# Attention scores of four images: from VectorE products to TensorE blocks with a masked sum, and a new order of an image's turn

## The chip, the cores and the metric

The kernel runs on one core of one Trainium2 chip. The metric is device time in microseconds (us) of one execution, the median over runs. In the text, PE is TensorE (PEld its weight loads), DVE is VectorE, ACT is ScalarE, POOL is GpSimd, SP is SyncE, which issues most transfers.

## The reference, cut to what matters

Four images of 784 patches become tokens of 256 features. The tokenizer puts the same tokens three times in a row (`REP = 3`). Then come two layers, each with an attention and a feed-forward part, all in float32. The change touches the attention of layer 0 alone. There the scores are taken between *images*, summed over all positions:

```python
mn = (m - mu) * jax.lax.rsqrt(var + EPS) * gamma + beta
q = (mn @ Wq).reshape(N, L, H, C)          # N images, L tokens, H = 8 heads of C = 32
k = (mn @ Wk).reshape(N, L, H, C)
v = (mn @ Wv).reshape(N, L, H, C)
g = jax.nn.sigmoid(mn @ Wg + bg).reshape(N, L, H, C)
att = jnp.einsum('slhc,tlhc->sth', q, k) * scale
att = jax.nn.softmax(att, axis=1)
o = jnp.einsum('sth,tlhc->slhc', att, v) * g
return o.reshape(N, L, H * C) @ Wo + bo
```

So for each pair of images (s, t) and each head, one number is the sum of 784 x 32 products. Behind it stand a mixture of six experts (two chosen for each token), a second attention and a second mixture.

## The kernel before, in words

**Stages.** The tokenizer runs first. Then, for eight groups `g` of three tiles of 128 tokens (group 0 has a fourth tile with the 16 left-over tokens of each image), `keys_values(g)` normalises the rows, turns them to features on partitions (`mT`), and projects them with `Wk` and `Wv`. After that each image `s` has a turn; the turns of images 0, 1 and 2 are a loop, image 3 is written out behind it. Then come the blocks of the experts (`hidden`, `rows_back`), the gathers, and layer 1.

**Order.** In these parts the order of PE, DVE and ACT is written by hand (`manual_schedule`): each engine works off its instructions in the program's order, and waits on semaphores for the other engines. PSUM tiles of one pool of seven banks are used in rotation.

**Keys and queries.** `projected(g, Wk, kT)` multiplies with a 128 x 128 piece of `Wk` as the stationary operand and 384 tokens as the moving one, so keys lie with features on partitions (`kT`, in the buffer `kq`). `q_mm` and `q_copy` do the same for the queries of one image, in halves of 392 tokens, two of them for each half `o` of the features (four heads each).

**Scores.** `products(s, o, ts)` multiplies on DVE the queries of image s with the keys of image t (128 x 784) and sums along the tokens by `accum_out`: one instruction for each o and t, 32 in all. `weights_of_images(s)` multiplies the sums by a matrix of head blocks on PE (tile `pl`), and makes the softmax over the images on DVE and ACT.

**A turn of image s.** `gate_mm` (16 PE records, tile `pg`) and `gate_act` make the gates with Tanh; `first_value` and `values` add up the weighted values of the four images on DVE into `oT`; `attended` projects pairs of tiles with `Wo` (tile `pwo`), adds them to the residual `h` on DVE and sums squares on ACT. The image before (u = s - 1) is routed in the same turn: `scales_of` (square root), `shifts_of`, `rows_of_part` (normalised rows `xn`), `turn_part` (12 transposes `pt`), `router` and `router_logits` (`pr`, `plg`), `choose` (18 small DVE instructions), `count` (`pcount`) and `send` (12 scatters on POOL). `mix1` to `mix3` belong to the image before that. The queries of image s + 1 are made in the turn of s.

**Behind it.** The expert weights `ew` (six transfers on SP, L1443) take the place of `kq` in SBUF, so they wait for the last reader of `kq`. `own_weights` copies one expert's weights out of `ew` (L1360) for each block of tokens.

**TensorE records.** A float32 matmul leaves two records in the trace, a transpose one.

Of the kernel before, what the change touches and what calls it, by code (L numbers as in the profile page):

```python
# [21 lines left out]
F32 = mybir.dt.float32  # L22
# [5 lines left out]
P = 128  # L28
# [18 lines left out]
PW = 4  # L47
SEG = 32
HALF = SEQ // 2
E0 = 6  # L50
E1 = 4
BLK = 256
# [16 lines left out]
def tile_vit_tower(ctx: ExitStack, tc: tile.TileContext, a: dict, out: bass.AP):  # L69
# [215 lines left out]
    def mm_t(n, w, wcols, xT, name, chunks=2):  # L285

        pm = ps_tile(name)
        for c in range(chunks):
            nc.tensor.matmul(  # L289
                pm[: wcols.stop - wcols.start, :n], w[:, c, wcols], xT(c),  # L290
                start=(c == 0), stop=(c == chunks - 1),
            )
        return pm[: wcols.stop - wcols.start, :n]
# [470 lines left out]
    scale = REP / math.sqrt(CHEAD) / math.sqrt(REP * SEQ)  # L764

    keys = layer0.enter_context(tc.tile_pool(name="keys", bufs=1, reuse_waits="tile"))
    kq = keys.tile([P, 2 * TOK + 4 * SEQ], F32, tag="kq", name="kq")
    kT = kq[:, : 2 * TOK].rearrange("p (c n) -> p c n", c=2)
    qT2 = kq[:, 2 * TOK :].rearrange("p (s c n) -> p s c n", s=2, c=2)
# [6 lines left out]
    pqs, pgs = {}, {}  # L776
    scatters = []

    def q_mm(s, o):
        if s >= NI:  # L780
            return
        pqs[s, o] = [
            mm_t(
                HALF, Wq, slice(o * P, (o + 1) * P),
                lambda c: mT[:, c, s * SEQ + i * HALF :][:, :HALF], "pq",
            )
            for i in range(2)
        ]

    def q_copy(s, o):  # L790
        if s >= NI:
            return
        if o == 0:
            qTs[s] = qT2[:, s % 2]
        for i, pq in enumerate(pqs.pop((s, o))):
            nc.scalar.copy(qTs[s][:, o, i * HALF : (i + 1) * HALF], pq)  # L796

    def gate_mm(s, o):
        pgs[s, o] = [
# [7 lines left out]
    def gate_act(s, o):  # L807
        gate = gates[s, o] = attr.tile([P, SEQ], F32, tag="gate", name="gate")
        for i, pg in enumerate(pgs.pop((s, o))):
            nc.scalar.activation(  # L810
                gate[:, i * HALF : (i + 1) * HALF], pg, AF.Tanh, bias=bgh[:, o : o + 1], scale=0.5
            )

    def products(s, o, ts=range(NI)):
        if s >= NI:
            return
        if s not in atts:
            atts[s] = small.tile([P, 2, NI], F32, tag="part", name="part")
        for t in ts:
            prod = attm.tile([P, SEQ], F32, tag="prod", name="prod")  # L820
            nc.vector.scalar_tensor_tensor(  # L821
                prod, qTs[s][:, o, :], 1.0, kT[:, o, t * SEQ : (t + 1) * SEQ],
                ALU.mult, ALU.mult, accum_out=atts[s][:, o, t : t + 1],
            )

    def weights_of_images(s):
        pl = psum_s.tile([P, 512], F32, tag="pss", name="pl")
        nc.tensor.matmul(
            pl[:, : 2 * NI], headmask, atts[s].rearrange("p o t -> p (o t)"),
            start=True, stop=True,  # L830
        )
# [12 lines left out]
    def first_value(s, o, n0, n, eng):  # L844
        if s not in oTs:
            oTs[s] = attr.tile([P, 2, SEQ], F32, tag="oT", name="oT")
        acc, v, w = oTs[s][:, o, n0 : n0 + n], vT[:, o, n0 : n0 + n], atts[s][:, o, 0:1]
        if eng is nc.scalar:
            nc.scalar.activation(acc, v, AF.Copy, scale=w)
        else:  # L850
            nc.vector.tensor_scalar(acc, v, w, None, ALU.mult)
# [358 lines left out]
    def projected(g, w, dst):  # L1210
        n = len(groups[g])
        t0 = groups[g][0]
        at = slice(t0 // TPI * SEQ + t0 % TPI * TT, t0 // TPI * SEQ + (t0 % TPI + 3) * TT)
        for o in range(2):
            pm = mm_t(
                n * TT, w, slice(o * P, (o + 1) * P),
                lambda c: firsts[0][:, c, :] if n > 3 else mT[:, c, at], "pkv",
            )
            nc.scalar.copy(dst[:, o, at], pm[:, : 3 * TT])  # L1219
            if n > 3:  # L1220
                nc.scalar.copy(left(dst[:, o, :]), left_of(pm[:, 3 * TT :]))

    def keys_values(g):
        projected(g, Wk, kT)
        if g + 2 < len(groups):
            stats = second_norm(g + 2)
        if g == 0:
            third[n - 1] = turned_rows(n - 1)
        turn_second(g + 1)
        projected(g, Wv, vT)  # L1230
        if g == 0:
            last_rows(n - 1)
        if g + 2 < len(groups):
            second_rows(g + 2, stats)

        t0 = groups[g][0]
        for ht, k in ((h[:, t0 : t0 + 3, :], 3), (h[:, LT:, :], 1))[: len(groups[g]) - 2]:
            nc.vector.tensor_tensor(ht, ht, over(bo, k), ALU.add)

    with tc.manual_schedule(engines=by_hand):  # L1240
        turn_second(0)
        last_rows(n - 2)
        second_rows(1, second_norm(1))
        keys_values(0)
        for g in range(1, len(groups)):
            keys_values(g)

            if g == 1:
                for o in range(2):
                    q_mm(0, o)  # L1250
                    q_copy(0, o)
            if g % 2 and g + 1 < len(groups):
                for o in range(2):
                    products(0, o, [g // 2])
    front.close()
    route = attention.enter_context(
        tc.tile_pool(name="route", bufs=1, side="right", reuse_waits="tile")
# [3 lines left out]
    with tc.manual_schedule(engines=by_hand):  # L1261
        for s in range(NI - 1):
            u = (s - 1, 0, TPI) if s else None
            past = (s - 2, 0, TPI) if s >= 2 else None
            if u:
                scales_of(u)
            if s == 0:
                for o in range(2):
                    products(0, o, [NI - 1])
                weights_of_images(0)  # L1270
            gate_mm(s, 0)
            gate_mm(s, 1)
            gate_act(s, 0)
            if s:
                products(s, 1, range(2))
            if u:
                shifts_of(u)
                rows_of_part(u)
                products(s, 1, range(2, NI))
            if s:  # L1280
                weights_of_images(s)
            if u:
                turn_part(u)
            first_value(s, 0, 0, SEQ, nc.vector)
# [149 lines left out]
    ew = keys.tile([P, E0, EW], F32, tag="kq", name="ew")  # L1434
# [817 lines left out]
```

## Time and profile before

| what | value |
|---|---|
| median of 3 runs | 784.22 us (781.89 to 785.8) |
| profiled execution: its time, its span | 785.9 us, 784.2 us |
| PE busy, DVE busy, ACT busy | 703.4, 480.2, 328.7 us |
| groups of keys and values | about 117 to 174.3 us of the span |
| turn of image 0, 1, 2 (first to last square root, `scales_of`) | from 174.3; 194.1 to 223.0; 223.0 to 253.7 |
| image 3 up to the first expert block | 253.7 to 286.0 us |
| expert blocks of layer 0 | 286 to 465 us |
| mean granted PE clock | 0.964 |

Starts in the trace are microseconds from the start of the span. "Busy" counts instructions at work; "idle before" is the wait of an engine in front of an instruction, with what ended it.

### The profile page before, as it was taken

What the parts mean: (1) busy time and instruction counts of PE and PEld (TensorE: products, weight loads), DVE (VectorE), ACT (ScalarE), POOL (GpSimd) and SP (SyncE); (2) the same over time, 40 slices, a digit from 0 to 9 for tenths busy, and PEclk for the clock granted to TensorE, in tenths of its full rate; (3) what the DMA queues carried; (4) which work ended last, traced back from release to release, by engine and by line L of the source; (5) the groups of instructions that cost most, each with busy time, mean ns of one, the idle gap of its engine ahead of it and who ended that gap; (6) DMA issues with size and microseconds to landing.
All of it is one profiled execution on the core that took longest, in us unless ns stands there. A gap on an engine that the chain in (4) does not pass through costs nothing.

```text
span 784.2 us, 10588 instructions
## 1 busy us (share of the span) xinstructions
PE 703.4 (90%) x3391; PEld 482.0 (61%) x3391; DVE 480.2 (61%) x1523; ACT 328.7 (42%) x777; POOL 129.2 (16%) x231
## 2 busy tenths in 40 slices
PE   6898899999888778998899999269999999999996
PEld 3745565666556456787788875146776775554653
DVE  4666886768778743446544766479965654454441
ACT  0545776455573652342222326135445613222221
POOL 5400000000064316500003027670000000000000
PEclk9999999999999789999999999779999999999999
DMA  8399999000021853432234252330000012223333
GB/s 189 99 415 418 418 415 416 6 1 1 0 82 40 289 187 110 141 94 76 88 95 121 94 156 75 88 100 8 1 0 1 1 24 93 82 63 102 104 112 105
DMA packets 56118, 96.24 MB, mean 123 GB/s; under 512 B 6376, under 2 KB 46031, under 8 KB 56063
## 3 DMA queue, kind: packets, MB, share of 16 engines
q1 hardware_dynamic: 49648, 79.38, 28.9%
q0 software_dynamic: 5536, 14.32, 6.0%
q10 hardware_dynamic: 878, 1.86, 1.0%
q8 instruction: 27, 0.44, 0.2%
q14 instruction: 29, 0.23, 0.1%
HBM read 30.45 MB, written 65.09 MB: 122 GB/s over the span
## 4 chain that ended last, share of the span: by engine, by line
PE 68%; DVE 16%; ACT 6%; issue 4%; DMA 3%; POOL 2%; DVEq 1%; ACTq 0%; another core or an unknown queue 0%; SPq 0%
PE pb L1384 11%; PE pe L289 6%; PE pyb L1402 5%; PE ps L289 4%; PE pqk L1828 4%; PE pkv L289 4%; PE pt L280 3%; PE pw L558 3%; PE pwp L300 3%; PE ps L2202 3%; PE pout L2002 2%; PE pout L2007 2%; DVE oT L856 2%; PE pukx L1927 2%; DMA img<-in_x_dram 2%
## 5 line engine op out<-in xcount | busy, mean ns | idle before, releaser
L1045 POOL DMA_INDIRECT xrows<-xn,pos x50 | 55.7, 1115 | 247.6 <-ACT kq L796 185.8
L1598 POOL DMA_INDIRECT ys<-yrows,pos x50 | 50.6, 1012 | 140.6 <-DMA yrows<-yb 123.9
L1384 PE MATMUL pb<-xTb,own 128*128 128x256 f32 (+1 forms) x240 | 56.0, 378 | 10.7 <-DVE own L1360 5.8
L1390 ACT ACTIVATE hb<-pb,own 128x256 f32<-128x256 f32 (+1 forms) x74 | 33.6, 456 | 62.7 <-PE pb L1384 50.4
L1384 PEld LDWEIGHTS pb<-xTb,own 128*128 128x128 f32 x240 | 42.3, 197 | 19.3 <-ACT hb L1390 8.5
L1384 PE MATMUL pb<-hb,own 128*128 128x256 f32 (+1 forms) x240 | 52.2, 360 | 0.8 <-DVE hb L1392 0.5
L1402 PE MATMUL pyb<-own,hb 128*128 128x256 f32 x216 | 52.6, 384 | 0.3 <-ACT hb L1390 0.2
L280 PE MATMUL pt<-ident,xn 128*128 128x128 f32 x200 | 34.8, 302 | 12.5 <-DVE xn L584 6.6
L289 PE MATMUL pe<-xT,eW 128*128 128x512 f32 (+1 forms) x112 | 46.0, 553 | 0.0
L1828 PE MATMUL pqk<-Wqkv,lxT 128*128 128x512 f32 x100 | 44.9, 594 | 0.2 <-ACT lxT L89 0.2
L1402 PEld LDWEIGHTS pyb<-own,hb 128*128 128x128 f32 x216 | 40.7, 193 | 6.5 <-ACT hb L1390 0.6
L1384 PEld LDWEIGHTS pb<-hb,own 128*128 128x128 f32 x240 | 40.5, 190 | 5.9 <-DVE hb L1392 1.2
L280 PEld LDWEIGHTS pt<-ident,xn 128*128 128x128 f32 x200 | 25.6, 151 | 28.2 <-ACT xn L919 8.5
L1408 DVE TENSOR_TENSOR yb<-pyb,eb 128x512 f32<-128x512 f32 (+1 forms) x30 | 19.1, 638 | 38.4 <-PE pyb L1402 28.1
L558 PE MATMUL pw<-Wall,pT 128*128 128x512 f32 x96 | 42.6, 593 | 0.0
L1373 ACT COPY xTb<-ptb 128x512 f32<-128x512 f32 (+1 forms) x30 | 16.2, 541 | 56.7 <-PE ptb L1369 49.9
L1392 DVE TENSOR_SCALAR hb<-pb,own 128x256 f32<-128x256 f32 (+1 forms) x46 | 20.6, 447 | 28.6 <-PE pb L1384 20.5
L1842 ACT ACTIVATE qk<-qk 128x256 f32<-128x256 f32 x50 | 20.4, 408 | 38.6 <-DVE qk L1834 35.0
L821 DVE SCALAR_TENSOR_TENSOR prod<-kq 128x784 f32<-128x784 f32 x32 | 30.4, 971 | 6.0 <-ACT kq L1219 3.4
L289 PEld LDWEIGHTS pe<-xT,eW 128*128 128x128 f32 x112 | 20.2, 190 | 21.6 <-issue 16.5
L1360 DVE COPY own<-ew 128x1540 f32 x30 | 28.9, 966 | 6.9 <-ACT xTb L1373 2.7
L1612 DVE SCALAR_TENSOR_TENSOR h<-ys,wk,h 128x256 f32<-128x256 f32 x50 | 23.5, 481 | 14.0 <-DMA ys<-yrows,pos 13.8
(414 smaller groups left out, 1463.5 us busy)
## 6 DMA issues: line engine op xcount, KB each, us to landing
xrows<-nothing SPq DMA_DIRECT2D x22, 896.0 KB
yrows<-nothing SPq DMA_DIRECT2D x22, 896.0 KB
out_dram<-h SPq DMA_DIRECT2D x23, 384.0 KB
xb<-xrows SPq DMA_DIRECT2D x24, 256.0 KB
yrows<-yb SPq DMA_DIRECT2D x24, 256.0 KB
ew<-in_L_ffn_expert_w_dram SPq DMA_DIRECT2D x6, 768.0 KB
wb<-wd SPq DMA_DIRECT2D x16, 128.0 KB
img<-in_x_dram SPq DMA_DIRECT2D x2, 588.0 KB
```

The lines of the kernel that those rows point to most:

```text
L280: nc.tensor.transpose(pt[:, j * TT : (j + 1) * TT], xn[:, j, c * P : (c + 1) * P], ident[:TT, :TT])
L289: nc.tensor.matmul(pm[: wcols.stop - wcols.start, :n], w[:, c, wcols], xT(c), start=(c == 0), stop=(c == chunks - 1),)
L300: nc.tensor.matmul(pm[:, i, :], xT(c, t), w[:, c, :], start=(c == 0), stop=(c == chunks - 1))
L558: nc.tensor.matmul(pm, pixels(c, tiles[j]), Wall[:, c, :], start=(c == 0), stop=(c == 1))
L821: nc.vector.scalar_tensor_tensor(prod, qTs[s][:, o, :], 1.0, kT[:, o, t * SEQ : (t + 1) * SEQ], ALU.mult, ALU.mult, accum_out=atts[s][:, o ...
L1045: put = nc.gpsimd.indirect_dma_start(out=xrows[:, :], out_offset=bass.IndirectOffsetOnAxis(ap=pos[:, k, t0 + j : t0 + j + 1], axis=0), in_ ...
L1360: nc.vector.tensor_copy(w, ewf[0][:, bass.ds(off, EW)])
L1384: nc.tensor.matmul(pm, wm[:, c, o * P : (o + 1) * P], src[:, c, :], start=(c == 0), stop=(c == 1),)
L1390: nc.scalar.activation(dst[:, o, :], pm, AF.Relu, bias=b)
L1402: nc.tensor.matmul(pm[:, t, :], src[:, c, t * P : (t + 1) * P], wm[:, c, :], start=(c == 0), stop=(c == 1),)
L1598: got = nc.gpsimd.indirect_dma_start(out=y[:, j, k, :], out_offset=None, in_=yrows[:, :], in_offset=bass.IndirectOffsetOnAxis(ap=pos[:, k, ...
L1828: nc.tensor.matmul(pqk, xTs[u][:, c, cut(j, 1)], Wqkv[:, c, : 2 * D], start=(c == 0), stop=(c == 1),)
```

## The change

Keys and queries are now made with *tokens* on partitions: seven chunks of 112 tokens for each image (`KC`, `NKC`), the chunk of `mT` as the stationary operand and the 256 columns of `Wk` or `Wq` as the moving one (`token_rows`). The scores become matmuls (`scores`): for each chunk and head, 32 columns of queries are stationary and the keys of all four images move (4 x 32 columns), so that PSUM holds a 32 x 32 block for each head and image t, of which only the diagonal is wanted. `score_sums` multiplies by a mask (`same`) and sums, on DVE. The loop's order is new: `weights_of_images(s)` stands behind the gate matmuls also for image 0, the queries of s + 1 stand ahead of the routing, `rows_of_part` shares its rows between ACT and DVE.

```diff
+KC = 112
+NKC = SEQ // KC
-    kq = keys.tile([P, 2 * TOK + 4 * SEQ], F32, tag="kq", name="kq")
+    kq = keys.tile([P, (NI + 1) * NKC * D], F32, tag="kq", name="kq")
+    def token_rows(s, ms, w, dst, name):
+        made = []
+        for m0 in ms[::2]:
+            two = [m for m in (m0, m0 + 1) if m in ms]
+            pm = ps_tile(name)[:KC].rearrange("p (t d) -> p t d", t=2)
+            for i, m in enumerate(two):
+                for c in range(2):
+                    nc.tensor.matmul(
+                        pm[:, i, :], mT[:, c, s * SEQ + m * KC :][:, :KC], w[:, c, :],
+                        start=(c == 0), stop=(c == 1),
+                    )
...
+    def scores(s):
+        ps = scored[s] = ps_tile("psc")[:, : 2 * NI * CHEAD]
+        for o in range(2):
+            for m in range(NKC):
+                for i in range(4):
+                    h0 = (4 * o + i) * CHEAD
+                    nc.tensor.matmul(
+                        ps[i * CHEAD : (i + 1) * CHEAD, o * P : (o + 1) * P],
+                        qrow[:, m, h0 : h0 + CHEAD], krow[:, :, m, h0 : h0 + CHEAD],
+                        start=(m == 0), stop=(m == NKC - 1),
+                    )
+    def score_sums(s):
...
+        nc.vector.tensor_tensor(own_, ..., same..., ALU.mult)
+        nc.vector.tensor_reduce(part.rearrange("p o t -> p (o t)"), own_, AX.X, ALU.add)
-    def products(s, o, ts=range(NI)):
...
     def keys_values(g):
-        projected(g, Wk, kT)
+        key_rows(g)
...
-            if g % 2 and g + 1 < len(groups):
-                for o in range(2):
-                    products(0, o, [g // 2])
+        scores(0)
+        score_sums(0)
...
             if u:
                 scales_of(u)
-            if s == 0:
-                for o in range(2):
-                    products(0, o, [NI - 1])
-                weights_of_images(0)
             gate_mm(s, 0)
             gate_mm(s, 1)
             gate_act(s, 0)
-            if s:
-                products(s, 1, range(2))
+            weights_of_images(s)
+            gate_act(s, 1)
             if u:
                 shifts_of(u)
-                rows_of_part(u)
-                products(s, 1, range(2, NI))
-            if s:
-                weights_of_images(s)
+                rows_of_part(u, both=True)
+            q_mm(s + 1, 0)
+            first_value(s, 0, 0, SEQ, nc.vector)
+            first_value(s, 1, 0, SEQ, nc.scalar)
+            q_copy(s + 1, 0)
             if u:
                 turn_part(u)
-            first_value(s, 0, 0, SEQ, nc.vector)
-            first_value(s, 1, 0, SEQ, nc.scalar)
-            gate_act(s, 1)
+            q_mm(s + 1, 1)
+            q_copy(s + 1, 1)
...
-            q_mm(s + 1, 0)
-            q_copy(s + 1, 0)
...
-            q_mm(s + 1, 1)
-            q_copy(s + 1, 1)
+            scores(s + 1)
             values(s, 1, 0, SEQ, range(1, 3))
...
             keep_left(s)
-            products(s + 1, 0, range(2))
-            for k, two in enumerate(halves(range(TPI))):
+            score_sums(s + 1)
+            for two in halves(range(TPI)):
                 attended(s, two)
-                if k < 2:
-                    products(s + 1, 0, [2 + k])
...
         gate_mm(s, 1)
         gate_act(s, 0)
-        products(s, 1, range(2))
+        weights_of_images(s)
         shifts_of(u)
         gate_act(s, 1)
-        products(s, 1, range(2, NI))
-        weights_of_images(s)
```

The queries of image 0 are still made behind group 1. `ew` takes the place of the smaller `kq`, whose last reader is now `scores(3)`, in the turn of image 2.

More of the change, by code (lines that the diff above doesn't have):

```diff
@@ L766, in tile_vit_tower @@
     keys = layer0.enter_context(tc.tile_pool(name="keys", bufs=1, reuse_waits="tile"))
-    kq = keys.tile([P, 2 * TOK + 4 * SEQ], F32, tag="kq", name="kq")
-    kT = kq[:, : 2 * TOK].rearrange("p (c n) -> p c n", c=2)
-    qT2 = kq[:, 2 * TOK :].rearrange("p (s c n) -> p s c n", s=2, c=2)
+    kq = keys.tile([P, (NI + 1) * NKC * D], F32, tag="kq", name="kq")
+    krow = kq[:KC, : NI * NKC * D].rearrange("p (t m d) -> p t m d", t=NI, m=NKC)
+    qrow = kq[:KC, NI * NKC * D :].rearrange("p (m d) -> p m d", m=NKC)
+    same = keys.tile([P, CHEAD], F32, tag="same", name="same")
+    nc.vector.tensor_reduce(
+        same, ident.rearrange("p (h c) -> p c h", c=CHEAD), AX.X, ALU.add
+    )
     att = ctx.enter_context(ExitStack())
@@ L775, in tile_vit_tower @@
     qTs, gates, atts, oTs, sums, rows0, turned0, logits0, picked, mixed = ({} for _ in range(10))
-    pqs, pgs = {}, {}
+    pqs, pgs, scored = {}, {}, {}
     scatters = []
-    def q_mm(s, o):
+    def token_rows(s, ms, w, dst, name):
[9 more added lines that the diff above has]
+                    )
+            made.append((dst[:, m0 : m0 + len(two), :], pm[:, : len(two), :]))
+        return made
@@ L780, in q_mm, with q_copy @@
+    def q_mm(s, part):
         if s >= NI:
             return
[L782 to L790, printed above, removed]
+        ms = range(4) if part == 0 else range(4, NKC)
+        pqs[s, part] = token_rows(s, ms, Wq, qrow, "pq")
+    def q_copy(s, part):
         if s >= NI:
             return
[L793 to L796, printed above, removed]
+        for dst, pm in pqs.pop((s, part)):
+            nc.scalar.copy(dst, pm)
@@ new lines, in scores @@
+    def scores(s):
+        if s >= NI:
+            return
+        ps = scored[s] = ps_tile("psc")[:, : 2 * NI * CHEAD]
[7 more added lines that the diff above has]
+                        start=(m == 0), stop=(m == NKC - 1),
+                    )
@@ new lines, in score_sums @@
+    def score_sums(s):
+        if s >= NI:
+            return
+        part = atts[s] = small.tile([P, 2, NI], F32, tag="part", name="part")
+        own_ = attm.tile([P, 2 * NI, CHEAD], F32, tag="ownc", name="ownc", bufs=1)
+        nc.vector.tensor_tensor(
+            own_, scored.pop(s).rearrange("p (k c) -> p k c", c=CHEAD),
+            same.unsqueeze(1).to_broadcast([P, 2 * NI, CHEAD]), ALU.mult,
+        )
+        nc.vector.tensor_reduce(part.rearrange("p o t -> p (o t)"), own_, AX.X, ALU.add)
@@ L811, in gate_act @@
                 gate[:, i * HALF : (i + 1) * HALF], pg, AF.Tanh, bias=bgh[:, o : o + 1], scale=0.5
-            )
-    def products(s, o, ts=range(NI)):
[L815 to L823, printed above, removed]
             )
@@ L1221, in projected, with key_rows @@
                 nc.scalar.copy(left(dst[:, o, :]), left_of(pm[:, 3 * TT :]))
+    def key_rows(g):
+        b, odd = divmod(g, 2)
+        for dst, pm in token_rows(
+            b, range(3, NKC) if odd else range(3), Wk, krow[:, b], "pkr"
+        ):
+            nc.scalar.copy(dst, pm)
     def keys_values(g):
-        projected(g, Wk, kT)
+        key_rows(g)
         if g + 2 < len(groups):
```

## The prediction

> **What bounds the kernel now.** I read the stretches by stage first, then each engine's instructions in order of time through one turn, then the row of the one tile that already uses quarters of the array. The stretches (length; busy time and instruction count of PE, PEld, DVE, ACT, POOL; clock, DMA share, GB/s):
>
> ```profile
> 117.00:174.34 57.34, 55.56 (x202) 33.54 (x200) 39.01 (x123) 31.68 (x71) 0.00 (x0) 1.00 0.36 149
> 194.14:223.00 28.86, 25.01 (x97) 16.89 (x96) 23.54 (x71) 16.91 (x38) 7.41 (x6) 0.94 0.07 23
> 223.00:253.70 30.70, 26.21 (x101) 16.86 (x100) 25.09 (x80) 17.29 (x41) 15.12 (x14) 0.94 0.15 53
> 285.96:465.00 179.04, 166.61 (x863) 141.24 (x863) 92.03 (x218) 55.32 (x120) 39.42 (x43) 0.98 0.33 104
> ```
>
> The groups of keys and values (first line) are PE's: 55.6 of 57.3 us. In the turns DVE is busy 23.5 of 28.9 us, but PE 25.0, so neither has much room. The expert blocks are PE's again, so a delay ahead of 286 us passes on to the end.
>
> Order of time, PE:
>
> ```profile
> 171.76 2.74 PE L289 MATMUL pkv<-mT,Wv 128*128 128x384 f32 x8
> 174.34 0.28 PE L828 MATMUL pl<-part,headmask 128*128 128x8 f32 x2
> 174.48 5.51 PE L289 MATMUL pg<-mT,Wg 128*128 128x392 f32 x16
> ...
> 202.10 2.92 PE L289 MATMUL pr<-xT,rw 128*128 128x512 f32 x8
> 205.14 1.50 PE L954 MATMUL plg<-rw,rT 128*128 128x6 f32 x12
> 206.50 2.88 PE L289 MATMUL pq<-mT,Wq 128*128 128x392 f32 x8
> ...
> 215.25 5.02 PE L300 MATMUL pwo<-Wo,oT 128*128 128x256 f32 x22 [1.32 <-DVE oT L861]
> ```
>
> `pl` starts the moment PE is through with the values, and the gates stand behind it. In turn 1, query matmuls fill PE while DVE chooses experts. Order of time, DVE:
>
> ```profile
> 177.17 0.63 DVE L851 TENSOR_SCALAR oT<-vT,att 128x784 f32<-128x784 f32 x1
> ...
> 206.68 0.20 DVE L974 TENSOR_TENSOR lg<-plg,rb 128x36 f32<-128x36 f32 x1
> ...
> 215.33 0.97 DVE L821 SCALAR_TENSOR_TENSOR prod<-kq 128x784 f32<-128x784 f32 x1
> ```
>
> The first value of turn 0 starts at 177.17. The choice starts at 206.68, 0.1 us behind the values of o = 0: DVE and the routing arrive together. The products stand between the last value and `attended`, where PE is busy with `pwo` anyway.
>
> **Prices.** A PE record costs its columns times 0.84 ns: 8 records of 384 took 2.58 us from start to start (171.76 to 174.34), so 256 columns cost 0.215 us, 392 cost 0.329. A product takes 0.895 us from start to start, so 32 of them 28.6 us, 24 of them in the turns.
>
> *The scores* are 112 records per image (56 matmuls), each 32 stationary columns by 128 moving. Four neighbours use four quarters of the array. Alone, a record would take 128 x 0.84 = 107 ns. The nearest row is the patch transpose, 32 by 112, also in fours:
>
> ```profile
> 23.69:32.40 8.71, 8.71 (x278) 8.37 (x278) 4.28 (x8) 0.80 0.24 22
> 32.54:35.84 3.30, 3.30 (x128) 3.09 (x128) 2.13 (x4) 1.00 0.02 5
> ```
>
> That is 31.3 ns a record at clock 0.80 and 25.8 ns at 1.00, where 112 columns alone would take 94: the quarters do overlap. Scaled by 128/112 it is 29.5 to 35.8 ns, so 3.3 to 4.0 us per image. I take 3.4, since PE is dense there. The upper bound, no overlap, is 12.0 us.
>
> **Part by part.**
>
> *Keys and queries.* In groups 1 to 7 the keys cost 8 records of 384 (2.58 us). Now it is 3 chunks in even groups (12 records of 256, 2.58) and 4 in odd ones (16, 3.44): +0.86 in four groups, +3.4 us. Group 0 gains nothing from its smaller work, because PE next waits there for DVE (0.71 us in front of the transposes). The queries of image 0 go from 16 x 0.329 = 5.27 to 28 x 0.215 = 6.02, +0.75. Against that stands one wait of 0.30 us that can shrink. Sum: +4, since PE sets this stage. The eight products here go for nothing: DVE is busy 39.0 of 57.3 us.
>
> *Scores of image 0.* They stand behind the last values on PE, with nothing beside them: +3.4. Their masked sum (about 0.4 + 0.36 us, from 256-wide rows of DVE such as 0.42) is hidden by the gates, which PE runs meanwhile.
>
> *The place of `pl`.* It now stands behind the 16 gate records: 16 x 0.329 = +5.3. DVE, with no image to route, has nothing else. From `pl` to the first value was 2.83 us (174.34 to 177.17), with an activation-table load of 1.28 in it; the table now loads ahead, for the gates: 1.75, so -1.1. The first value moves from 177.2 to 188.8 (+4, +3.4, +5.3, -1.1 = +11.6).
>
> *End of each turn.* From the last value (186.28) to the next square root (194.14) were 7.86 us: four products and three pairs of `attended` on DVE, then squares. Without products PE paces it: 0.15 to start, three pairs of `pwo` at 1.73, 0.28 to be seen, 0.88 for the last pair, 1.33 for two squares: 7.83. The products removed here give nothing. The masked sum (0.8) hides in the 2 us until the first pair is there.
>
> *Turn 1, square root to choice*: 12.54 us (194.14 to 206.68). Now, in the written order, ACT: square root with its table 1.59, table and two gate halves 2.25, exponent 0.12, two more halves 0.96, three rows instead of six 1.47; then PE: end of the transposes 1.35, second part of the queries (12 records) 2.58, router (2.58), and 1.68 to the end of the logits and their arrival. Sum 14.6: +2.1. ACT's `q_copy` ahead of its copies of `xT` lies inside the PE time of the queries. Queued behind the late logits are `choose`, the values of o = 1 and the next scores. DVE waits some 4 us there, which is where products would have been. Its three extra rows (1.05) fall into that wait.
>
> *Turn 1, choice to next square root*: 16.3 before. The scores (3.4) follow `pcount`, end about 1.2 us ahead of the last value, and are hidden; with 4.6 us or more they would be late. Unchanged.
>
> *Turn 2* adds `mix3` (0.5): 14.6 + 16.4 + 0.5 = 31.5, against 30.70 in the trace, where small work for the early blocks stood between products: +0.8.
>
> *Image 3.* From the square root to the first value were 6.20 (253.70 to 259.90). Its four products go, but `pl` waits for 16 gate records and the early-block matmuls between them, which ended in the old order after 6.0 us; they start 2.5 us ahead of the square root and `pl` to value takes 1.75, so about 5.8: -0.4.
>
> *Expert weights.* SP's six transfers waited for the last product (258.2). They now wait for `scores(3)`, which ends near 258.7 in the shifted time. The first copy out of `ew` stood at 284.85 with 14 us more now: no gain, except at most the 0.33 us that PE waited for `xb`. POOL's scatters start later with the turns and have the same 14 us.
>
> Sum: 4 + 3.4 + 5.3 - 1.1 + 2.1 + 0.8 - 0.4 = +14.1. The profiled execution took 785.9 (span 784.2); with the change 800.0. The median of the runs is 1.7 lower, so I predict **798**.
>
> [...] In this trace waits of 1.3 to 2.2 us went with a granted clock of 0.94 in the turns and 1.00 without waits. The new order has a PE wait of 3.2 us (logits to `pcount`), just ahead of the scores. [...] My sum leaves a slower clock at zero. From the rows I bound it at 0 to 3 us a turn: twice what 0.94 means there now (6% of 25 us of PE work is 1.5).
>
> **Rivals.** *The turns are DVE's (faster).* If DVE alone set the turns, 24 products (21.5 us) would go and four masked sums and six rows (5.1) come: -16.4, with +4 for the keys -12.4, so 772. For it: DVE runs nearly without a wait from 206.7 to 223. Against: PE needs 25 us of a turn already, and would get 0.75 + 3.4 more. It holds only if the logits come before the values of o = 0 end; the chain above puts them 4 us behind. 4%.
>
> *Gaps fill (no change).* If PE never waited, a turn with routing would be the sum of its records: gates 5.27, `pl` 0.25, queries 6.02, transposes 1.3, router 2.58, logits 1.36, counts 0.7, scores 3.4, `pwo` 5.2, together 26.1. Between the starts of the gates lie 28.93 and 29.88 (191.18, 220.11, 249.99): -2.8 and -3.8. Turn 0 has 20.1 against 16.84: +3.3. With the +4 and +3.4 ahead it is +4.1, and +0.5 if the four products of image 3 (3.6) come off whole: 785. For it: PE is 87% busy in turn 1. Against: `pwo` and the logits wait for work that itself waits for PE. 3%.
>
> *The quarters don't overlap (slower still).* 12.0 us of scores: +8.6 for image 0, about +8 in turn 0 and +7.4 in each of turns 1 and 2: +31, so 829. For it: here the four moving operands differ, there they are the same. Against: both are issued as matmuls of their own. 5%.
>
> **How the numbers follow.** The forecast, near +14, has 88%. Downward its unknowns are the 4 of the groups and the 2.9 of turns 1 and 2, which would vanish if waits hid them: +7, and less the 1.7 between this execution and the median +5.5, so 790. Upward they are the clock (3 in each of three turns) and scores at 4.0 instead of 3.4: +24, so 808. The range holds the forecast but for thin ends and leaves out the fast and the slowest rival and most of the second. A measurement of this kernel tells about 0.5% (3.9 us) from no change. Slower gets 88 + 5%, the same 3%, faster 4%.
>
> **What the new profile would show.** Right: `psc` records at about 30 ns; `pl` of image 0 near 187 behind the gates; first value near 189; square roots near 205.6, 236.7, 268; DVE idle some 4 us in front of the choice, ended by `plg`; `pwo` pacing `attended`; the first expert block near 300. Wrong: a choice that follows the values at once, `psc` at 100 ns, or a first value ahead of 184.

## The result and the profile after

The changed kernel took a median of **820.4 us** (four executions, 816.06 to 824.83) against 784.34 of the kernel before (four, 781.89 to 785.8): a ratio of **1.045, interval 1.040 to 1.050**. The profiled execution took 819.25 (span 817.5). 798 was predicted, with a range to 808: slower, but by 36 us instead of 14.

The stretches that answer to those of before (length; busy time and instruction count of PE, PEld, DVE, ACT, POOL; clock, DMA share, GB/s), the end of the keys and values, turn 1, turn 2, the expert blocks:

```profile
117.00:177.71 60.71, 59.67 (x262) 43.06 (x260) 31.32 (x106) 32.52 (x69) 0.00 (x0) 1.00 0.34 138
204.21:246.76 42.55, 37.06 (x240) 27.32 (x239) 18.53 (x61) 15.47 (x34) 11.66 (x12) 0.88 0.11 38
246.76:284.63 37.87, 26.49 (x202) 20.63 (x200) 19.42 (x64) 15.89 (x37) 11.49 (x12) 0.82 0.29 100
320.38:499.40 179.02, 166.16 (x866) 141.97 (x866) 92.72 (x219) 55.21 (x121) 38.67 (x43) 0.98 0.33 105
```

The keys and values grew from 57.34 to 60.71, the expert blocks not at all (179.04 to 179.02). The loss is in turns 1 and 2: 42.55 and 37.87 us instead of 28.86 and 30.70. DVE does less work there than before (18.5 us instead of 23.5) and has 24 us of nothing in turn 1. Order of time on DVE, from the first value of image 0 on:

```profile
187.83 0.63 DVE L879 TENSOR_SCALAR oT<-vT,att 128x784 f32<-128x784 f32 x1
...
218.71 0.20 DVE L1002 TENSOR_TENSOR lg<-plg,rb 128x36 f32<-128x36 f32 x1 [3.68 <-PE plg L982]
...
227.19 0.18 DVE L897 COPY oL<-oT 128x32 f32<-128x32 f32 x1
236.07 0.42 DVE L832 TENSOR_TENSOR ownc<-psc,same 128x256 f32<-128x256 f32 x1 [8.71 <-PE pwo L302]
...
241.00 0.42 DVE L913 SCALAR_TENSOR_TENSOR h<-pwo,h 128x256 f32<-128x256 f32 x1 [4.04 <-remote]
```

Up to the choice of experts (218.71) the times are near the forecast. Then DVE waits 8.71 us for the scores and 4.04 for the first attention output. The same stretch on PE:

```profile
222.40 0.64 PE L1052 MATMUL pcount<-tiles,allones 128*128 128x36 f32 x2 [0.29 <-DVE tiles L1033]
222.98 4.85 PE L821 MATMUL psc<-kq 112*32 112x128 f32 x104
228.13 0.44 PE L821 MATMUL psc<-kq 112*32 112x128 f32 x6 [0.31 <-issue]
228.86 0.40 PE L821 MATMUL psc<-kq 112*32 112x128 f32 x2 [0.29 <-issue]
229.19 5.23 PE L302 MATMUL pwo<-Wo,oT 128*128 128x256 f32 x23
```

By its records PE was through with the scores at 229.26 and with the first pair of `pwo` near 231. DVE went on 6.8 and some 10 us later. So by these records the wait is not for PE's work but for PE's *signal* of it; such a signal is called late below. "issue" and "remote" say that the profile shows nothing that would have held the engine. Gaps marked "issue" run through PE's records until 243. Beside this, GpSimd sends the rows of image 0 to the experts (`send`): 12 scatters, the first at 226.10, the last at 240.15. The same lies over the end of turn 2 and the start of image 3.

### The profile page after: what moved, and what is told of

Read it like the earlier page. It is cut to its first block, busy times and chain, and to the rows that moved or that the text cites. A ratio compares the mean times of both kernels' runs of the same rounds, so it can differ in the third digit from the quotient of the medians.

```text
span 817.5 us, 11609 instructions
## 1 busy us (share of the span) xinstructions
PE 727.1 (89%) x3935; PEld 513.3 (63%) x3935; DVE 457.7 (56%) x1474; ACT 326.6 (40%) x769; POOL 123.5 (15%) x231
## 4 chain that ended last, share of the span: by engine, by line
PE 74%; DVE 13%; issue 4%; ACT 3%; POOL 2%; another core or an unknown queue 1%; DMA 1%; DVEq 1%; ACTq 0%
PE pb L1409 11%; PE pe L291 5%; PE pyb L1427 5%; PE ps L291 4%; PE pqk L1851 4%; PE pt L282 4%; PE pw L560 3%; PE pwp L302 3%; PE pwo L302 3%; PE pg L291 3%; PE ps L2225 3%; PE pkr L793 3%; PE pout L2025 2%; PE pout L2030 2%; PE pkv L291 2%
## 5 line engine op out<-in xcount | busy, mean ns | idle before, releaser
L1073 POOL DMA_INDIRECT xrows<-xn,pos x50 | 50.0, 999 | 277.2 <-DVE pos L1070 198.3
L282 PE MATMUL pt<-ident,xn 128*128 128x128 f32 x200 | 31.0, 286 | 16.1 <-ACT xn L947 9.2
L282 PEld LDWEIGHTS pt<-ident,xn 128*128 128x128 f32 x200 | 23.8, 144 | 29.1 <-ACT xn L947 11.5
L919 ACT ACTIVATE junk<-h,nm 128x256 f32<-128x256 f32 x25 | 12.7, 507 | 58.0 <-DVE nm L917 52.1
L1635 DVE SCALAR_TENSOR_TENSOR h<-ys,wk,h 128x256 f32<-128x256 f32 x50 | 23.3, 478 | 14.1 <-DMA ys<-yrows,pos 13.7
```

What stands on the lines that cost most here:

```text
L282: nc.tensor.transpose(pt[:, j * TT : (j + 1) * TT], xn[:, j, c * P : (c + 1) * P], ident[:TT, :TT])
L1073: put = nc.gpsimd.indirect_dma_start(out=xrows[:, :], out_offset=bass.IndirectOffsetOnAxis(ap=pos[:, k, t0 + j : t0 + j + 1], axis=0), in_ ...
```

## The experiments

Each series ran on a chip of its own, beside the kernel before. That kernel took 785 to 788 us on three of them (called slower chips here; the first results, at 784, are like them) and 777 on two (faster chips). So a difference that goes with the chip can't be told from one that goes with the occasion; "chip" below stands for both. Ratios are to the kernel before in the same series. Turn 1 and turn 2 are the times from square root to square root.

The changed kernel itself ran in three series:

| kernel | kernel before | ratio, interval | turn 1, turn 2 (us) |
|---|---|---|---|
| changed, first result | 784.3 | 1.045 (1.040 to 1.050) | 42.55, 37.87 |
| changed, after_again | 788.5 | 1.045 (1.038 to 1.052) | 43.90, 39.79 |
| changed, after_third | 776.8 | 1.017 (1.015 to 1.020) | 32.52, 31.65 |

### Without the scatters of turns 1 and 2, on both kernels (slower chip)

```diff
-        for j in range(n):
+        for j in range(n if b >= 2 else 0):
             for k in range(2):
                 put = nc.gpsimd.indirect_dma_start(
```

> The changed kernel without the 24 scatters of rows of images 0 and 1 (in the turns of images 1 and 2); it leaves these rows of the experts' input unwritten. Theory S (while GpSimd's scatters run, TensorE's signals and instructions come late: in the profile VectorE waits 8.7 us for scores that TensorE had done): the waits of 8.7 and 4 us go, turn 1 falls from 42.6 to about 31.0 us and turn 2 from 37.9 to about 31.5, as the prediction's sum had them, and the time is about 800 us. Theory C (the slower TensorE clock, which follows TensorE's wait of some 3 us for the choice of experts): the scatters do not matter, turn 1 stays above 40 us and the time near 820.

> The kernel before without the same 24 scatters, as the counterpart; it leaves these rows unwritten. Theory S: the old turns hid the late signals behind VectorE's products, so 0 to 3 us are gained: 781 to 784 us. Theory C: no difference, 784 us. If it gained as much as the changed kernel does, the scatters would not be what the change runs into.

The changed kernel fell to 800.73 us, ratio 1.017 (1.011 to 1.022). Turns 1 and 2 took 32.57 and 31.67. The kernel before stayed at 785.81, ratio 0.998 (0.995 to 1.001). DVE at the end of turn 1, without the scatters:

```profile
228.82 0.42 DVE L832 TENSOR_TENSOR ownc<-psc,same 128x256 f32<-128x256 f32 x1 [1.75 <-PE psc L821]
230.71 0.42 DVE L913 SCALAR_TENSOR_TENSOR h<-pwo,h 128x256 f32<-128x256 f32 x1 [1.00 <-PE pwo L302]
```

8.71 became 1.75, 4.04 became 1.00. Theory S holds: what lies over the prediction comes from the scatters, which cost nothing in the turns of the kernel before. Theory C falls for these 20 us. The changed kernel itself is not in this series, but this run is its own control: the scatters of image 2, behind the turns, were kept, and there a signal is late. The records of `pr` end at 312.89, and ACT reads it at 318.18, 5.3 us later.

### Which PE work has to meet the scatters (slower chip)

`a_few_scores` issues one of seven chunks of the scores of images 1 to 3; `a_scores_early` moves `scores(s + 1)` from behind `count(u)` to behind `router_logits(u)`:

```diff
-            for m in range(NKC):
+            for m in range(NKC if s == 0 else 1):
```

> The changed kernel with one of the seven chunks of the scores of images 1 to 3: 16 records of TensorE instead of 112 at the same place, the scatters as they are. The scores of these images are then sums over 112 tokens. Theory S in the form that a dense block of records running into the scatters makes the backlog: the waits go, turn 1 takes 29 to 31 us, time 797 to 800 us. Theory S in the form that scatters hold back TensorE's signals whatever it runs: turn 1 stays near 40 us, time 814 to 820. Theory C: the wait in front of the scores is still there and so is the slow clock, but fewer records pay for it: 812 to 818.

```diff
                 router_logits(u)
+            scores(s + 1)
             values(s, 0, 0, SEQ)
...
                 count(u)
-            scores(s + 1)
```

> The changed kernel with the scores of image s + 1 issued ahead of the choice of experts instead of behind the counts, so that they run in TensorE's wait of some 3 us and are over before the first scatter. Theory S, dense block: no backlog, turn 1 takes 29 to 31 us, time 795 to 800 us. Theory S, scatters alone: the signals of the attention output are late as before, time 812 to 818. Theory C: the wait is filled, so the clock stays up, time 795 to 800.

813.03 (1.031, 1.025 to 1.037) and 811.15 (1.031, 1.024 to 1.039). Both forms of theory S are half right, and none of their forecasts of the time was met. (813.03 would fit theory C's 812 to 818, but a late `pl` is no part of theory C.) Turn 1 fell to 31.98 and 32.87, so a dense block of scores that runs into the scatters is what made turn 1 so long. Turn 2 stayed at 36.64 and 37.61: with the scores out of the way it is `pl` whose signal is late at its start (DVE waits 8.42 and 7.53 us there, 4.41 where signals are on time), and behind turn 2 the small matmuls of `early_blocks`.

`a_few_scores` also shows the clock: with little on PE in turn 0, it waits 2.94 us, and the attention output behind that wait takes 7.83 us where 22 records took 5.02 at a granted clock of 1.00 in the changed kernel (196.83 to 201.85). By the two times that is an estimate of 0.64 for the clock; the mean of the whole execution was 0.943, against 0.956 there:

```profile
196.68 7.83 PE L302 MATMUL pwo<-Wo,oT 128*128 128x256 f32 x22 [2.94 <-DVE oT L889]
```

### Four edits at once on another chip (faster)

`a_dve_busy` adds four long DVE products (result unused) where the old ones stood at the end of a turn, `a_warm` eight PE records in the wait for the choice, `a_half_sends` leaves out every second scatter, `b_new_scores` has the new scores in the old order.

```diff
+            again(2)
             score_sums(s + 1)
             for k, two in enumerate(halves(range(TPI))):
                 attended(s, two)
+                if k < 2:
+                    again(1)
```

> The changed kernel with four added VectorE products of 128 x 784 (their result is not used) at the end of each turn of images 0 to 2, at the places of the old ones: two behind the last value, one behind each of the first two pairs of attention output. Theory V (VectorE's long products slowed the scatters and so let TensorE's signals through; without them the scatters run at full pace and the signals wait): scatters come further apart than 1.27 us, the late signals go, turn 1 falls from 42.6 to 34 to 37 us, and the time is 805 to 814 in spite of 11 us more VectorE work. If VectorE's work does not matter: turn 1 as long or up to 2 us longer, 819 to 826.

```diff
                 router_logits(u)
+                for _ in range(2):
+                    mm_t(HALF, Wg, slice(0, P), lambda c: mT[:, c, s * SEQ :][:, :HALF], "pdum")
```

> The changed kernel with eight added TensorE records of 392 columns (2.6 us, result not used) behind the logits, in TensorE's wait for the choice of experts in turns 1 and 2, so that the granted clock should not fall ahead of the scores. Theory C2 (the slow clock is what makes the collision: the scores then run into the scatters): scores take 3.3 us instead of some 6, turn 1 falls to 31 to 33 us, the time to 800 to 808. If the scatters do it at any clock: the signals stay late, and only the 2 to 3 us of the slow scores are saved in each turn: 813 to 819.

```diff
-            for k in range(2):
+            for k in range(2 if b >= 2 else 1):
                 put = nc.gpsimd.indirect_dma_start(
```

> The changed kernel with 6 instead of 12 scatters in each of turns 1 and 2 (the rows' second experts are left out). They are through about 8 us after the first. If the price goes with the number of scatters: about 810 us. If what counts is that they meet the end of the scores: the signal of the scores comes when the scatters end, near 234 instead of 236, and the rest of turn 1 is free: 803 to 808. If a single scatter is enough: 815 to 820.

> The new keys, queries, scores and masked sums in the old order of a turn (weights of the images ahead of the gates for image 0; queries of the next image in the wait for the choice and behind the counts; the scores of image s + 1 behind these queries, ahead of the attention output). By sums from the trace: +4 keys and queries, +3.4 scores of image 0, and at the end of each turn the scores stand on the path in front of the attention output, some 4 us in each of three turns: about 803 us if TensorE's signals come in time. If the collision with the scatters needs only the new scores and not the new order: 812 to 820.

They took 791.13 (1.018), 787.86 (1.015), 788.49 (1.015) and 790.12 us (1.017), and none had a late signal. That looks like four cures; but the kernel before had become faster too, 776.91. No row of these runs could tell a cure from a chip on which nothing needs one. So this series settles nothing about late signals, and `a_half_sends` was not run again. It does price two things where signals are on time. With the wait filled, the scores take what the sum had, 3.27 us, about as long as in turn 0 of the changed kernel (3.26 at 192.62, at a granted clock of 1.00). Rows of `a_warm` and of the changed kernel on a faster chip (after_third, where the granted clock was 0.81 from 217.10 to 235.20):

```profile
221.74 3.27 PE L821 MATMUL psc<-kq 112*32 112x128 f32 x112
```

```profile
221.41 6.02 PE L821 MATMUL psc<-kq 112*32 112x128 f32 x112
```

Its turns took 30.64 and 30.66 instead of 32.52 and 31.65. In the total the gain can't be told apart (1.013 to 1.017 against 1.015 to 1.020). And the new scores in the *old* order cost as much as in the new one on a faster chip (1.015 to 1.020): there DVE waits for the scores in every turn (4.01 us in turn 0), here the queries stand ahead of the choice.

### The changed kernel beside its variants (slower chip)

> The changed kernel itself once more, beside the kernel before. In the last four runs the kernel before took 777 us where it had taken 785, and no signal of TensorE came late in any of the four, whatever they changed. Theory P (the late signals are a matter of the chip the run was on): where the kernel before takes about 777, the changed kernel takes 789 to 793 (ratio 1.016 to 1.021), turns 1 and 2 take 31 to 32 us with all scatters; where it takes 785, the changed kernel takes about 820. Theory K (each of the four edits took the late signals away): the ratio is 1.04 to 1.05 on any chip, and turn 1 takes 40 us or more.

> The kernel with TensorE records in the wait for the choice of experts once more, now beside the changed kernel itself. Where signals come in time: scores of 3.3 us instead of 5 to 6, turns of 30.6 us, 2 to 4 us under the changed kernel. Where they come late (kernel before at 785): if the slow clock makes the collision, 800 to 808, else 813 to 819.

822.88 us: the first result again, 1.045. `a_warm_again` took 812.26 (1.029, 1.024 to 1.034) where the same kernel had 1.015 on the faster chip: as theory P has it, the late signals go with the chip. Its scores took 3.26 us and turn 1 30.37, but turn 2 37.18. Filling the wait removes the collision of the scores in turn 1, not the late signals behind it; theory C2 is wrong on the total, though 812.26 lies just under the other forecast, too.

`a_pl_first` restores the old place of `pl` for image 0:

```diff
+            if s == 0:
+                weights_of_images(0)
             gate_mm(s, 0)
             gate_mm(s, 1)
             gate_act(s, 0)
-            weights_of_images(s)
+            if s:
+                weights_of_images(s)
```

> The changed kernel with the weights of the images ahead of the gate matmuls for image 0, as in the kernel before. By the prediction's step (pl behind the 16 gate records costs +5.3, the earlier table gives back 1.1) the first value comes about 4 us earlier and the time falls by as much. Rival: the turn of image 0 is TensorE's own (gates 5.3, queries 6, scores 3.3, attention output 5.2 us, nearly without a wait), so the early first value only makes VectorE wait for the scores at the end: 0 to 1 us.

The first value came at 183.30 instead of 188.08, and it helped nothing: 827.64 us (1.049, 1.042 to 1.056), the first square root at 205.66 instead of 205.76. DVE ran ahead and then waited for the scores; PE has no gap between `pl` and the attention output:

```profile
181.63 0.39 PE L856 MATMUL pl<-part,headmask 128*128 128x8 f32 x2 [1.00 <-DVE part L836]
181.88 5.51 PE L291 MATMUL pg<-mT,Wg 128*128 128x392 f32 x16
187.23 6.21 PE L793 MATMUL pq<-Wq,mT 128*112 128x256 f32 x28
193.36 3.26 PE L821 MATMUL psc<-kq 112*32 112x128 f32 x112
196.56 5.45 PE L302 MATMUL pwo<-Wo,oT 128*128 128x256 f32 x24
```

The rival holds: turn 0 is PE's own.

`a_queries_late` puts the second part of the queries into the wait for the choice:

```diff
-            q_mm(s + 1, 1)
-            q_copy(s + 1, 1)
             if past:
                 mix1(past)
             if u:
                 router(u)
                 router_logits(u)
+            q_mm(s + 1, 1)
+            q_copy(s + 1, 1)
```

> The changed kernel with the second part of the queries (12 records, 2.6 us) behind the logits, in TensorE's wait of 3.2 us for the choice, instead of ahead of the router. By the prediction's chain from square root to choice, 2.6 us come off each of turns 1 and 2 (14.5 to about 12), and the clock does not fall ahead of the scores: 5 to 8 us under the changed kernel. If the values of o = 0 set the choice instead, less than 2 us a turn.

> The changed kernel with the second part of the queries behind the logits, once more. Where the kernel before takes 785 to 788: 1.023 of it again. Where it takes 777: the changed kernel took 788.8 there, and the edit takes 2.6 us and the slow clock (1.8 us of scores) from each of turns 1 and 2: 780 to 784, a ratio of 1.004 to 1.010.

Both series fell on slower chips: 809.73 (1.023, 1.017 to 1.029) and 805.14 (1.022, 1.018 to 1.025). That is 13 us under the changed kernel in the first of the two, more than expected, because turn 1 no longer collides: 29.09 and 29.08 us, as short as before (28.86). The chain from square root to choice itself fell from 14.5 to 13.2, half of the 2.6 expected: PE now waits for ACT's copies of the transposed rows,

```profile
212.59 2.85 PE L291 MATMUL pr<-xT,rw 128*128 128x512 f32 x8 [1.04 <-ACT xT L961]
```

and the rest of the gain is scores of 3.27 us, where the changed kernel took 6.28 in its first result (222.98 to 229.26). Signals are late again at the start of turn 2 (9.94 and 8.55 us in front of `mx<-pl`), so it stays slower than before. What it gives on a faster chip was not measured. No version of these runs beats the kernel before.

### Why the turns of the kernel before have no late signals

The kernel before has the same scatters. What differs beside them is DVE. `b_short_products` cuts the products of the kernel before from 784 tokens to 32, and changes nothing else:

```diff
-                prod, qTs[s][:, o, :], 1.0, kT[:, o, t * SEQ : (t + 1) * SEQ],
+                prod[:, :CHEAD], qTs[s][:, o, :CHEAD], 1.0, kT[:, o, t * SEQ :][:, :CHEAD],
```

Faster chip first, with the changed kernel and `a_dve_busy` beside it:

> The changed kernel as it is, as the counterpart of the two others on the same chip. Where the kernel before takes 785 to 788: 820 to 825, turn 1 of 42 to 44 us. Where it takes 777: 789 to 793, turn 1 of about 31 to 32 us, if the late signals are a matter of the chip; 812 if they are not.

> The changed kernel with four added long VectorE products at the end of each turn of images 0 to 2 (result not used), on a chip to be compared with the changed kernel itself. Where the kernel before takes 785 to 788: theory V (long products of VectorE keep the scatters from holding up TensorE's signals) gives turn 1 of 33 to 37 us and 803 to 812 us; if VectorE's work is not what matters, 820 to 828. Where it takes 777: about 791, which tells nothing on this.

> The kernel before with each of its 32 products cut to 32 of the 784 tokens: the same instructions, semaphores and order, but VectorE idle for some 0.8 us where each product stood (the scores are sums over 32 tokens only). Where the kernel before takes 785 to 788: theory V gives late signals in its turns, waits of 2 to 10 us in front of pl or pwo, and 790 to 808 us in spite of less work; without V it is 780 to 788. Where the kernel before takes 777: 770 to 777.

The changed kernel took 788.76, the kernel before 776.77: **+12.0 us, ratio 1.017**. `a_dve_busy_again` took 791.49 (1.021, 1.018 to 1.024) and the short products 773.77 (0.995, 0.992 to 0.997). Then a slower chip:

> The kernel before with its products cut to 32 of 784 tokens, once more. Where the kernel before takes 777: 0.995 of it again (773). Where it takes 785 to 788: theory V (long products of VectorE keep the scatters from holding up TensorE's signals) gives waits of 2 to 10 us in front of pl or pwo and 790 to 808 us in spite of less work; without V 780 to 785.

> The changed kernel with four added long VectorE products at the end of each turn of images 0 to 2 (result not used), once more. Where the kernel before takes 777: 791 again. Where it takes 785 to 788: theory V gives turn 1 of 33 to 37 us and a ratio of 1.020 to 1.030 to the kernel before (803 to 812 us); if VectorE's work is not what matters, 1.045 or more (820 to 828).

**Less work was slower**: the short products took 795.56, ratio 1.008 (1.005 to 1.011), where they had gained half a per cent. **More work was faster**: the changed kernel with four added products a turn took 800.91, ratio 1.017 (1.013 to 1.022), against 1.045 without them in the two other series on slower chips. The changed kernel itself did not run on this chip, but `a_queries_late_again` did, and its DVE waited 8.55 us for `pl` at the start of turn 2. With the added products that wait is 4.30, and turns 1 and 2 take 31.81 and 32.30, better than forecast:

```profile
230.62 0.42 DVE L922 SCALAR_TENSOR_TENSOR h<-pwo,h 128x256 f32<-128x256 f32 x1 [0.49 <-issue]
239.46 0.17 DVE L872 TENSOR_REDUCE mx<-pl 128x2 f32<-128x8 f32 x1 [4.30 <-issue]
```

Theory V holds on both sides. The short products left turn 1 as it was (29.28 us, no late signal); turn 2 took 32.85 instead of 30.70. DVE in the kernel before with short products, slower chip, from the start of turn 2 on:

```profile
231.50 0.17 DVE L835 TENSOR_REDUCE mx<-pl 128x2 f32<-128x8 f32 x1 [6.28 <-PE pt L280]
...
259.17 0.15 DVE L1075 COPY place<-pplace 78x1 f32<-78x1 f32 x1 [3.45 <-remote]
264.15 0.17 DVE L1087 TENSOR_TENSOR meta<-pmeta,shift 1x21 int32<-1x21 f32 x1 [4.38 <-remote]
```

and the row of the first wait in the kernel before as it was (with short products on a faster chip it was 0.65):

```profile
227.39 0.17 DVE L835 TENSOR_REDUCE mx<-pl 128x2 f32<-128x8 f32 x1 [0.54 <-PE pl L828]
```

So on slower chips the products had two jobs: the scores, and keeping PE's signals on time. GpSimd's rows show what they do to the scatters. Scatters of the kernel before (start, length), and two of the products beside them:

```profile
215.44 1.73 POOL L1045 DMA_INDIRECT xrows<-xn,pos  x1 [0.30 <-issue]
217.47 0.96 POOL L1045 DMA_INDIRECT xrows<-xn,pos  x1 [0.30 <-issue]
218.00 0.97 DVE L821 SCALAR_TENSOR_TENSOR prod<-kq 128x784 f32<-128x784 f32 x1
218.74 1.06 POOL L1045 DMA_INDIRECT xrows<-xn,pos  x1 [0.31 <-issue]
219.78 0.97 DVE L821 SCALAR_TENSOR_TENSOR prod<-kq 128x784 f32<-128x784 f32 x1
220.11 1.47 POOL L1045 DMA_INDIRECT xrows<-xn,pos  x1 [0.30 <-issue]
221.89 1.47 POOL L1045 DMA_INDIRECT xrows<-xn,pos  x1 [0.30 <-issue]
```

and of the changed kernel:

```profile
228.77 0.96 POOL L1073 DMA_INDIRECT xrows<-xn,pos  x1 [0.30 <-issue]
230.03 0.96 POOL L1073 DMA_INDIRECT xrows<-xn,pos  x1 [0.30 <-issue]
```

A scatter that starts while a product is under way is lengthened, mostly to 1.28 to 1.74 us, by about what is left of the product (0.51 us at 220.11, where 0.64 were left). One that starts ahead of the product is not (217.47). In the changed kernel nearly all take 0.96 and follow each other every 1.27 us. What holds such a scatter back, no run here shows. That the lengthening goes with *faster* kernels is measured: on slower chips 1.017 with four added products a turn against 1.045 without, and 1.008 with the products of the kernel before cut short.

It is only in its turns that the kernel before has no late signals. Behind them, beside the scatters of image 2 (289.71 to 305.31), there are no products, and its own trace on the slower chip has:

```profile
299.23 1.45 PE L289 MATMUL pr<-xT,rw 128*128 128x384 f32 x4
304.16 0.58 ACT L943 ACTIVATE rT<-pr,cols 128x384 f32<-128x384 f32 x1 [4.64 <-issue]
```

ACT reads `pr` 3.5 us after its records end. In `b_short_products`, on a faster chip, the same step follows after 0.1 us:

```profile
294.44 1.45 PE L289 MATMUL pr<-xT,rw 128*128 128x384 f32 x4
295.99 0.58 ACT L943 ACTIVATE rT<-pr,cols 128x384 f32<-128x384 f32 x1 [2.60 <-PE pr L289]
```

What stays open: why a row of scatters holds up PE's signals, and only on some chips. In `a_dve_busy_third` only three of the twelve scatters of turn 1 were lengthened much (1.65, 1.29 and 1.48 us), and all signals came in time, those beside unlengthened scatters too. So a simple "one slow scatter, one signal" is not it. Whether it is the spacing of the scatters or something else about a busy DVE wasn't separated.

## Why the prediction was right and wrong

**The sum was near where nothing is late, in part by luck.** +14.1 was forecast; the changed kernel took +12.0 where the kernel before takes 776.8, and a ratio of 1.017 on a slower chip without the 24 scatters. The first expert block, forecast near 300, starts at 320.38 in the first result, at 296.65 on a faster chip and at 298.01 without the scatters.

Step by step, with the first result's rows:

- *Keys and queries*, +4: `psc` starts at 177.71 where `pl` had started at 174.34, so +3.4: right, a little high.
- *Scores*: 112 records in 3.26 us, 29 ns each, as forecast, against the estimate of 107 for a record alone. The quarters of the array overlap; that rival is out.
- *`pl` behind the gates*, +5.3 less 1.1: it came at 186.27 and the first value at 187.83 (forecast 187 and 188.8). But the step is wrong as a cause. `a_pl_first` took the 5 us away and the turn ended at the same time. Turn 0 is a row of PE work (20 us), and the chain of the first value only happened to be as long. The sum of +11.6 came out at +10.1 (square root at 205.51 against 195.43), and that is luck: what the row of PE work gives is 3.4 for keys and queries, 3.3 for the scores of image 0 and the +3.3 that the rival *Gaps fill* had for turn 0.
- *Turn 1, square root to choice*, 14.6: 14.50 (204.21 to 218.71), with DVE idle 3.68 us, ended by `plg`. The sum was right, but not every term is worth its full length: with the 2.6 us of queries moved away the chain fell by 1.3, because copies on ACT were next.
- *Turn 1, choice to square root*, "unchanged", 16.4: it took 28.05 (218.71 to 246.76). This is where it failed, for two reasons. The smaller is the clock, left at zero with a bound of 0 to 3 us a turn: behind PE's waits of 1.52, 0.66 and 0.29 us the granted clock was 0.73 while the scores ran (222.98 to 229.26), where it was 1.00 in turn 0 (192.62 to 195.88). In after_third (waits of 1.52, 0.89 and 0.53 us; clock 0.81 from 217.10 to 235.20) scores of 3.4 took 6.0, and DVE waited 1.7 us for them. On the faster chips it cost 1.9 us in turn 1 and 1.0 in turn 2 (32.52 and 31.65 against 30.64 and 30.66 with the wait filled), inside the bound: +2.9 for both turns. How long a wait it takes to lower the clock was not shown.
- *The rest of turns 1 and 2 and image 3*: against a faster chip, 42.55 instead of 32.52, 37.87 instead of 31.65 (without the scatters on a slower chip 32.57 and 31.67), and 10.04 instead of 5.25 from square root to first value of image 3: **+21 us of late signals**.

The ledger closes: 3.4 + 6.7 up to the first square root (10.1), turn 1 +13.7, turn 2 +7.2, image 3 +3.8 make 34.8; the first expert block moved by 34.4, and 1.1 came back behind it, against 33.35 between the two profiled executions.

**The step that failed** is "without products PE paces it ... the products removed here give nothing", together with "POOL's scatters start later with the turns and have the same 14 us". Work was costed at nothing when it went, because its own time was hidden. What was not asked is what the engine does to its neighbours while it works. The prediction looked at when the scatters end, not at what they run beside: after the change they lie beside PE signals for which DVE waits with nothing else to do. The turns of the trace of before could not show the price, since products and scatters ran together there. Its expert blocks did show a sign: the last 3.5 of the 4.64 us for which ACT waited for `pr`, beside the scatters of image 2, with nothing in the profile to explain them. That could have given the range a term upward; it had none.

**The rivals.** *The turns are DVE's* is out by direct measurement: cutting all 32 products to a twenty-fourth of their length gains 0.5% on a faster chip. *Gaps fill* is out too: even on a faster chip the time rose by 12.0 us, and PE waits at the choice (1.52, 0.66 and 0.29 us in turn 1).

## What to carry to other kernels

Before taking hidden work away, list what runs beside it on the other engines, and ask who will now wait there with nothing to do: work that costs no time may be what keeps a transfer from colliding with a signal (here the kernel before took 1.008 of its time with its products cut short, on a slower chip). When a wait ends long after the record it waited for, leave out the transfer beside it before blaming the engine named. And run the kernel itself in the same series as its variants: on a chip that lacks the trouble, every edit looks like a cure (here four edits at 1.015 to 1.018, and the changed kernel itself at 1.017).

## What was not expected of the hardware

- By its records PE had finished the scores at 229.26, and DVE saw it at 236.07, 6.8 us later, while GpSimd issued one scatter after another, every 1.27 us. Without the scatters DVE's wait there fell from 8.71 to 1.75.
- It goes with the chip (or the occasion): the same changed kernel was 1.045 of the kernel before in two series and 1.017 in another. The kernel before itself took 777 us on two chips and 785 to 788 on three.
- On a slower chip the kernel before got slower with less DVE work (1.008), and the changed kernel faster with more of it (1.017, against 1.045 in two other series on slower chips).
